# Two reductions of the second masked attention, moved in front of the dense attention's shares in VectorE's order

## The chip, the cores and the metric

The kernel runs on one core of a Trainium2 chip, with one launch. The metric is the time of one execution in device microseconds (us). Five engines work side by side, each through its own instructions in order: TensorE (PE; its weight loads are listed as PEld), VectorE (DVE), ScalarE (ACT), GpSimd (POOL) and SyncE (SP), which issues most of the DMA transfers. They wait for each other through semaphores.

## The reference

Sixteen batches of 1024 nodes with 256 features go through two layers of graph attention, each with a layer norm in front and a residual around it. Layer 0 holds an MLP, an attention over all nodes ("dense"), a second MLP and an attention masked by the adjacency matrix; layer 1 is one masked attention. Cut to what matters here:

```python
def _gat(inp, adj_mask, W, a):           # layer 0, slope 0.2; dense where adj_mask is None
    h = jnp.matmul(inp, W)
    f1, f2 = jnp.matmul(h, a[:F_, 0]), jnp.matmul(h, a[F_:, 0])
    e = jax.nn.leaky_relu(f1[:, :, None] + f2[:, None, :], ALPHA)
    if adj_mask is not None:
        e = jnp.where(adj_mask[None, :, :] > 0, e, NEG_INF)
    att = jax.nn.softmax(e, axis=2)
    return jax.nn.elu(jnp.einsum('bij,bjf->bif', att, h))
...
# layer 1, slope 0.01
h = jnp.matmul(inp, W)
e_src, e_dst = jnp.einsum('bnf,f->bn', h, a1), jnp.einsum('bnf,f->bn', h, a2)
e = jax.nn.leaky_relu(e_src[:, :, None] + e_dst[:, None, :], negative_slope=ALPHA)
e = jnp.where(adj[None, :, :] == 0, NEG_INF, e)
h_prime = jnp.matmul(jax.nn.softmax(e, axis=-1), h)
```

## The kernel before

**Order by a table.** All work is cut into small steps. Each step is entered in a table with a due time by `at(lo, hi, steps)`, which spreads the steps evenly from `lo` to `hi`. The due times are planned microseconds, and only their order counts: at the end the table is sorted by due time and the steps are issued one after the other, which fixes the order of instructions on PE, DVE, ACT and SP. POOL is kept in the same order by dependencies, with its scatters free among themselves. A step that issues nothing on an engine doesn't change that engine's order.

**Batches overlap.** Every batch `b` has a base, `base_of(b)`, 142 planned units after the one before (28 less from batch 1 on). Around one base the loop plans, for the middle batches: the layer 0 masked attention of batch `b` (`masked_first`, class `Gnn0`, tiles named with an a: `hma`, `exta`), the norm and the projections of the layer 1 masked attention of batch `b` (`second_norm`, class `Gnn1`, tiles named with a b: `hmb`, `extb`), the end of the dense attention of batch `b+1` (`dense_end`, class `Dense`), the first MLP and dense projections of batch `b+2`, and the first norm of batch `b+3`. The layer 1 attention proper (`masked_second`) comes one base later.

**The dense attention** doesn't multiply out its 1024 x 1024 weights (batch 0 does for half of its rows). The nodes are sorted by one of their two scores, sums from the front and from the back of the sorted rows are put into a fine and a coarse table in DRAM, and for every node POOL gathers one row of each table by an indirect DMA (L637; the coarse row is added to the fine one on landing). Per half of a batch (four tiles of 128 nodes) `share` (four DVE instructions, L649 to L652) makes the denominators from the gathered rows `got`. Then `mean`, once for each of the four tiles, scales the front sums on ACT (L659, tile `part`, two buffers) and adds the back sums on DVE (L661, tile `hp`). `merge` transposes the four `hp` tiles on PE (L708) for each of four column blocks, applies the first two steps of the elu on DVE and ACT (L710 to L712), and `merge_end` adds the result to `resT` (L718 on DVE, L719 on POOL).

**The layer 1 attention's preparation.** `project` multiplies each of eight node tiles with the weights on PE (L322) and copies the result from PSUM to `hmb` on ACT (L324). `extremes` reduces column 1 of `hmb`, the second scores, to their maximum and minimum for each partition (L329 and L330 on DVE, tile `ext`). `vectors` spreads the maximum over the partitions with a transpose on PE (L238, PSUM tile `extps`, from one of two `tr` buffers, which `merge` uses too), reduces it again on DVE (L339), and makes the exponentials of the attention on DVE and ACT (L341 to L351).

For a middle batch the order around the change, in planned units after `base_of(b)`: projections of layer 1 from 71 to 77.1; `share` of the first half at 78 and its four `mean` at 78.2, 78.575, 78.95 and 79.325; four steps of the first MLP (`mlp1`, L451, two products each, relu L454 on ACT) at 78.1, 79.85, 81.6 and 83.35; `extremes` at 78.5; `vectors` at 82; `merge` of the first half from 85, with projections of the dense attention (L465) between.

Of the kernel before, what the change touches and what calls it, by code (L numbers as in the profile page):

```python
# [31 lines left out]
def fast_path(ctx: ExitStack, tc: tile.TileContext, alarm, x, adj, w1, b1, w2, b2, w_fc, a_fc,  # L32
# [189 lines left out]
    def at(lo, hi, steps):  # L222
        for i, step in enumerate(steps):
            table.append((lo + (hi - lo) * i / len(steps), len(table), step))
# [543 lines left out]
    def each(f, *ranges):  # L768
        out = [()]
        for r in ranges:  # L770
            out = [o + (i,) for o in out for i in r]
        return [partial(f, *o) for o in out]
# [117 lines left out]
    def last(b, n=1):  # L890
        return b >= NB - n

    def second_norm(t0, b):
        n, m = norm2[b], gnn1[b]
        if last(b):
            n.turn_at(t0 + 46.5, 0)
            n.turn_at(t0 + 49, 1, 1.6)
            lo = t0 + 50
        elif b == 0:
            n.turn_at(t0 + 47, 0)  # L900
            n.turn_at(t0 + 50.5, 1, 1.6)
            lo = t0 + 47.2
        else:
            n.turn_at(t0 + 60.3, 0, 7)
            n.turn_at(t0 + 67.3, 1)
            lo = t0 + 71
        at(lo, lo + 7, each(m.project, range(NT)))
        at(lo + 7.5, lo + 7.5, [m.extremes])
        if last(b, 2):
            at(lo + 7.8, lo + 7.8, [m.vectors])  # L910
            at(lo + 8.2, lo + 8.2, [m.row])
            at(lo + 8.3, lo + 9.5, each(m.scale, range(NT)))
        else:
            at(lo + 11, lo + 11, [m.vectors])
            at(lo + 24, lo + 24, [m.send])
            at(lo + 40, lo + 52, each(m.scale, range(NT)))
            at(base_of(b + 1) - 4.5, base_of(b + 1) - 4.5, [partial(m.row, True)])
# [22 lines left out]
    def base_of(b):  # L940
        return b * PERIOD - SHORT * (b > 0)
# [37 lines left out]
    for t in range(TH):  # L979
        lo = START + 95 + 7.1 * t  # L980
# [31 lines left out]
    for b in range(NB):  # L1012
        base, after_base = base_of(b), base_of(b + 1)
        masked_first(base, b)
        second_norm(base, b)
        if last(b):
            parts = [base + 65 + 7 * q for q in range(NQ)]
        elif last(b, 2):
            parts = [base + 86, base + 94.5, base + 107.5, after_base + 39]
        else:  # L1020
            parts = [after_base + lo for lo in (11, 46, 53, 60)]
        masked_second(parts, b)
        if b + 1 < NB:
            if b:
                dense_sums(base, b + 1)
            for h in range(NH):
                if b:
                    gathers(dense[b + 1], h, base + 44.5 + 3.5 * h, base + 55 + 7 * h)
                else:
                    gathers(dense[1], h, base + 16 + 12 * h, base + 22 + 25 * h)  # L1030
            dense_end(after_base - PERIOD, b + 1)
        if b + 2 < NB:
            first_mlp(base, b + 2)
            dense_rows(after_base - PERIOD, b + 2)
            dense_begin(after_base, b + 2)
        if b + 3 < NB:
            lo = after_base - PERIOD + 86
            at(lo, lo, [partial(load_first, b + 3)])
            first_norm(after_base, b + 3)
# [465 lines left out]
```

## Time and profile before

| | |
|---|---|
| time, median of 4 runs | 2360.46 us (2358.52 to 2362.2) |
| profiled execution | 2356.86 us, its span 2355.1 us, granted clock 0.991 |
| PE busy | 2263.6 us, 96% |
| DVE busy | 1611.6 us, 68% |
| ACT busy | 1242.8 us, 53% |
| POOL busy | 954.3 us, 41% |
| two reductions of layer 1, L329 and L330 | 16 times each, 159 and 156 ns (medians) |
| the transpose of their result, L238 | 16 times, 294 ns (median) |

The span runs from the first to the last instruction of the program. The chain of waits, which follows the work that ended last back from the last instruction, is spread over many lines. Its largest shares are PE 8% and DVE 4%, and the largest line is L384, a product of the masked attention, with 2%. The table of waits is read as: the engine, tile and line that waited, the engine, tile and line (or DMA) that released it, the total, the number of times and the longest. The timeline gives the start and the duration in us of instructions of the same kind put together, with the idle time before them and its releaser in brackets. PE's rows have modelled ends. "Granted clock" is the share of TensorE's full clock that the chip's throttle let through.

### The profile page before, as it was taken

The numbers are of one execution on the slowest core, as the hardware profiler recorded it, in microseconds if no ns is written. First come the engines' busy times: TensorE is split into PE (matmuls) and PEld (weight loads), VectorE is DVE, ScalarE is ACT, GpSimd is POOL, SyncE is SP. The second block draws the span as 40 slices with busy tenths as digits, with TensorE's granted clock in tenths as the row PEclk, the third lists the DMA queues.
The fourth block names the chain that finished last, engine by engine and source line by source line (L and its number), as shares of the span: only waits on it lengthen the run. The fifth ranks groups of instructions, "written<-read, shape, count | busy, mean of one in ns | idle before, by whom it ended". The sixth has DMA issues, their size and how long they took to land. (4 is left out here: it accounts for less than half of the span.)

```text
span 2355.1 us, 30815 instructions
## 1 busy us (share of the span) xinstructions
PE 2263.6 (96%) x9955; PEld 1749.6 (74%) x9955; DVE 1611.6 (68%) x4499; ACT 1242.8 (53%) x2740; POOL 954.3 (41%) x1216
## 2 busy tenths in 40 slices
PE   8989999999999999999999999999999999999897
PEld 6667777777868778787777868777786877868666
DVE  6666685766858667775866868576685856768554
ACT  5345645547355563745547365564736556373442
POOL 1153435264433536335263533526443353634320
PEclk9999999999999999999999999999999999999899
DMA  4557346562655736366573645657265574636500
GB/s 173 168 155 212 72 162 179 163 186 91 199 133 175 184 136 182 100 185 163 169 196 104 194 116 165 176 168 191 97 197 120 175 184 145 181 90 202 127 1 29
DMA packets 150763, 355.81 MB, mean 151 GB/s; under 512 B 11113, under 2 KB 62649, under 8 KB 146497
## 3 DMA queue, kind: packets, MB, share of 16 engines
q0 software_dynamic: 45952, 163.99, 26.2%
q1 hardware_dynamic: 103968, 189.58, 26.2%
q8 instruction: 82, 1.34, 0.2%
q14 instruction: 89, 0.72, 0.1%
q10 hardware_dynamic: 672, 0.17, 0.0%
HBM read 227.40 MB, written 126.30 MB: 150 GB/s over the span
## 5 line engine op out<-in xcount | busy, mean ns | idle before, releaser
L384 PE MATMUL ob<-hmb,attb 128*128 128x257 f32 x2048 | 463.3, 384 | 13.8 <-DVE attb L373 13.8
L465 PE MATMUL h<-wfc_sb,resT 128*128 128x257 f32 x2048 | 465.8, 380 | 0.0
L384 PE MATMUL oa<-hma,atta 128*128 128x258 f32 x2048 | 455.8, 383 | 2.8 <-DVE atta L373 2.6
L384 PEld LDWEIGHTS ob<-hmb,attb 128*128 128x128 f32 x2048 | 386.2, 191 | 78.0 <-ACT rb L422 12.4
L384 PEld LDWEIGHTS oa<-hma,atta 128*128 128x128 f32 x2048 | 388.6, 190 | 64.7 <-DVE atta L373 8.0
L465 PEld LDWEIGHTS h<-wfc_sb,resT 128*128 128x128 f32 x2048 | 379.5, 190 | 53.5 <-issue 0.7
L719 POOL TENSOR_TENSOR resT<-resT,e 128x512 f32<-128x512 f32 x128 | 163.1, 1275 | 384.2 <-DVE e L718 340.9
L408 POOL TENSOR_TENSOR posa<-posa,onat 128x256 f32<-128x256 f32 x120 | 100.8, 840 | 469.2 <-ACT posa L400 468.6
L373 DVE SCALAR_TENSOR_TENSOR atta<-rowsa,qwda,edge 128x256 f32<-128x256 f32 x512 | 267.9, 553 | 25.6 <-PE oa L384 14.3
L373 DVE SCALAR_TENSOR_TENSOR attb<-rowsb,qwdb,edge 128x256 f32<-128x256 f32 x512 | 236.8, 505 | 8.4 <-PE ob L384 5.8
L451 PE MATMUL m<-hT,w_sb 128*128 128x512 f32 x512 | 237.3, 602 | 0.5 <-ACT posa L400 0.5
L726 PE MATMUL m<-resT,w_sb 128*128 128x512 f32 x512 | 231.2, 598 | 4.4 <-POOL resT L719 4.4
L422 ACT ACTIVATE rb<-ob,recb 128x256 f32<-128x256 f32 x128 | 59.0, 474 | 329.2 <-DVE recb L420 326.6
L637 POOL DMA_INDIRECT got<-coarse,k x124 | 198.0, 1597 | 38.5 <-issue 34.8
L399 ACT ACTIVATE ea<-oa,reca 128x256 f32<-128x256 f32 x128 | 60.7, 474 | 269.6 <-DVE reca L396 269.6
L710 DVE TENSOR_SCALAR e<-hpT 128x512 f32<-128x512 f32 x128 | 88.4, 690 | 139.4 <-PE hpT L708 106.9
L726 PEld LDWEIGHTS m<-resT,w_sb 128*128 128x128 f32 x512 | 94.1, 192 | 106.9 <-issue 91.2
L451 PEld LDWEIGHTS m<-hT,w_sb 128*128 128x128 f32 x512 | 93.4, 194 | 92.9 <-issue 90.6
L637 POOL DMA_INDIRECT got<-fine,k x124 | 128.9, 1040 | 54.1 <-issue 23.1
L525 POOL DMA_INDIRECT sorted<-hnat,place x128 | 131.4, 1026 | 39.6 <-issue 21.4
L548 ACT ACTIVATE junk<-r,fs 128x1024 int8<-128x1024 f32 x124 | 142.4, 1148 | 6.8 <-issue 3.6
L711 ACT ACTIVATE e<-e 128x512 f32<-128x512 f32 x128 | 80.7, 631 | 86.2 <-DVE e L710 86.1
(186 smaller groups left out, 3441.5 us busy)
## 6 DMA issues: line engine op xcount, KB each, us to landing
xs<-sorted SPq DMA_DIRECT2D x32, 1028.0 KB
fine<-tt SPq DMA_DIRECT2D x32, 1026.0 KB
fine<-xs SPq DMA_DIRECT2D x32, 1026.0 KB
x<-in_x_dram SPq DMA_DIRECT2D x16, 1024.0 KB
out_dram<-x SPq DMA_DIRECT2D x32, 512.0 KB
xn<-in_x_dram SPq DMA_DIRECT2D x15, 1024.0 KB
coarse<-carry SPq DMA_DIRECT2D x32, 256.5 KB
r<-row_r SPq DMA_DIRECT2D x14, 512.0 KB
```

The lines of the kernel that those rows point to most:

```text
L373: nc.vector.scalar_tensor_tensor(a_t, self.rows[:, q * PAIR:(q + 1) * PAIR], self.qwd[:, 1, j:j + 1], edge[:, j, q * PAIR:(q + 1) * PAIR], ...
L384: nc.tensor.matmul(self.out[t][:, :F + self.ONES], lhsT=self.att[q, j][:, (t % 2) * P:(t % 2 + 1) * P], rhs=self.hm[:, j, 2:2 + F + self.O ...
L408: adder.tensor_add(pos, pos, o_nat[:, t, :])
L451: nc.tensor.matmul(ps, lhsT=w1_sb[:, kc, c * P:(c + 1) * P], rhs=hT[:, kc, h * HALF:(h + 1) * HALF], start=(kc == 0), stop=(kc == FC - 1))
L465: nc.tensor.matmul(ps[:, :F + 1], lhsT=self.resT[:, kc, t * P:(t + 1) * P], rhs=wfc_sb[:, kc, g, :], start=(kc == 0), stop=(kc == HC - 1))
L525: made = nc.gpsimd.indirect_dma_start(out=sorted_d[self.b % 2], out_offset=bass.IndirectOffsetOnAxis(ap=self.place[:, t:t + 1], axis=0), i ...
L548: nc.scalar.activation(junk, self.r2, AF.Sign, bias=self.fs[:, 0, t:t + 1], accum_out=self.signs[:, t:t + 1])
L637: nc.gpsimd.indirect_dma_start(out=got[u // n][:, u % n, :], out_offset=None, in_=(coarse_d if coarse else fine_d)[self.b % 2][:, :], in_o ...
L710: nc.vector.tensor_scalar_min(e, ps, 0.0)
L711: nc.scalar.activation(e, e, AF.Exp)
L719: nc.gpsimd.tensor_add(dst, dst, e)
L726: nc.tensor.matmul(ps, lhsT=w2_sb[:, kc, c * P:(c + 1) * P], rhs=self.resT[:, kc, h * HALF:(h + 1) * HALF], start=(kc == 0), stop=(kc == H ...
```

## The change

The due time of `extremes` in `second_norm` goes from 7.5 to 6.9 units after `lo`, where `lo` is 71 units after the base for batches 1 to 14, 47.2 for batch 0 and 50 for batch 15. The projections that it reads keep due times up to 6.125 after `lo`. `extremes` of the layer 0 attention, planned in `second_mlp`, is not touched.

```diff
         at(lo, lo + 7, each(m.project, range(NT)))
-        at(lo + 7.5, lo + 7.5, [m.extremes])
+        at(lo + 6.9, lo + 6.9, [m.extremes])
         if last(b, 2):
             at(lo + 7.8, lo + 7.8, [m.vectors])
             at(lo + 8.2, lo + 8.2, [m.row])
```

## The prediction

> **What bounds the kernel.** I read the page first. TensorE (PE) is busy for 2263.6 of 2355.1 us, 96%, VectorE (DVE) for 68%; the chain of waits names mostly PE lines. So a change pays only where it shortens a PE wait, or what PE meets next. The table of waits (columns: engine, tile and line that waited, what released it; total us, times, longest) has two rows that bear on this step:
>
> ```profile
> DVE den L649 <- DMA got<-coarse,k: 133.6, 26, 10.7
> ...
> PE extpsb L238 <- DVE extb L330: 21.5, 14, 3.0
> ```
>
> PE waits 21.5 us for the second reduction of `extremes` (L330). Inside 300 to 2100 us it is 19.9 us in 12 waits, the largest PE row there; the next is 8.0 us. VectorE itself stands for 133.6 us at the first instruction of `share` (L649), waiting for gathered rows. The reductions are queued behind that. One round (batch 1) in the timeline, start and duration first:
>
> ```profile
> 378.59 5.31 PE L451 MATMUL m<-hT,w_sb 128*128 128x512 f32 x12
> 378.79 0.37 ACT L324 COPY hmb<-pb 128x258 f32<-128x258 f32 x1 [0.50 <-PE pb L322]
> ...
> 383.52 0.17 DVE L649 TENSOR_TENSOR den<-got,qd 128x4 f32<-128x4 f32 x1 [9.91 <-DMA got<-coarse,k]
> ...
> 385.08 0.75 DVE L661 SCALAR_TENSOR_TENSOR hp<-got,den,part 128x513 f32<-128x513 f32 x1 [0.79 <-ACT part L659]
> 385.75 0.16 DVE L329 TENSOR_REDUCE extb<-hmb 128x1 f32<-128x8 f32 x1
> 385.83 0.15 DVE L330 TENSOR_REDUCE extb<-hmb 128x1 f32<-128x8 f32 x1
> ...
> 386.06 0.29 PE L238 MATMUL extpsb<-ident,extb 128*128 128x128 f32 x1 [2.16 <-DVE extb L330]
> ```
>
> The last input of the reductions, ScalarE's (ACT's) copy at L324, is there at 379.16 (378.79 + 0.37). PE ends its twelve matmuls at 383.90, and sits 2.16 us. The next stretch decides the matter:
>
> ```profile
> 385.90 2.29 DVE L661 SCALAR_TENSOR_TENSOR hp<-got,den,part 128x513 f32<-128x513 f32 x3
> 386.19 1.88 PE L451 MATMUL m<-hT,w_sb 128*128 128x512 f32 x4
> ...
> 387.91 0.67 PE L708 MATMUL hpT<-ident,hp 128*128 128x128 f32 x4
> ```
>
> After the transpose of the extremes PE has one `mlp1` step (1.88 us), and then the transposes of `merge`, one for each `mean` result. The fourth result ends at 385.90 + 2.29 = 388.19, and the fourth transpose starts at 388.25. In twelve of the thirteen rounds of this kind (batches 1 to 13) it starts 0.05 to 0.07 us after that end. So PE reaches the two waits almost together: it is already bound by `mean` two microseconds later.
>
> **What the step moves.** Only two reductions, with no DMA and nothing on another engine. In batches 1 to 13 the new due time (77.9 instead of 78.5 after the base) puts them in front of four instructions of `share` (78.0) and one of `mean` (78.2). In batches 0, 14 and 15 no VectorE step lies between the two due times (in 14, `share` comes ten units later), so nothing changes there. On PE, ACT, POOL and SP the order stays.
>
> **Cost on VectorE.** The two take 0.16 and 0.15 us, overlapped 0.23. They gain a wait of their own, for the last copy of `project`. Behind it are queued `share` and `mean`, and PE waits for these. But the copy is done before the gathers in every round: 379.16 against 383.52 here, 1080.18 against 1082.34 in batch 6, the narrowest. VectorE is idle then. So the cost is nothing, hidden by the wait for the gathers; without that cover it would be 0.23 us a round, 3.0 us in all. Batch 14 shows the step with nothing in front: copy ready 2190.46, reduction 2190.49, PE's transpose 2190.80, so 0.34 us later. At 379.16 + 0.34 = 379.5 the extremes are ready 4.4 us before PE comes at 383.90. The wait at L238 goes wholly: 2.16, 2.06, 2.97, 1.00, 0.44, 0, 0.29, 1.47, 1.77, 1.99, 2.30, 1.93 and 1.56 us in batches 1 to 13, together 19.9.
>
> **What is late next.** PE runs its `mlp1` step from about 384.0 and is at `merge` at 385.9, two microseconds early. The results it transposes come from `share`, which the gathers release, and these don't move: in the stretch before it the DMA engines are full, as the row of the windows shows (us, busy time of PE, weight loads, DVE, ACT, POOL, then clock, DMA share, GB/s):
>
> ```profile
> 379.20:383.50 4.30, 4.30 (x11) 1.72 (x10) 0.00 (x0) 0.69 (x1) 2.40 (x3) 1.00 1.07 226
> ```
>
> What moves is only that the reductions no longer stand between the first `mean` and the second. From the start of the first to the end of the fourth that takes now 388.19 - 385.08 = 3.11 us. The nearest row without them is the other half, later in the same round, the same four instructions unbroken:
>
> ```profile
> 399.00 2.97 DVE L661 SCALAR_TENSOR_TENSOR hp<-got,den,part 128x513 f32<-128x513 f32 x4 [1.47 <-ACT part L659]
> ```
>
> 3.11 - 2.97 = 0.14 us. The reductions took 0.23, but the scale on ACT that feeds each `mean` sets the pace after the second. So the fourth transpose comes 0.14 us earlier, and the rest of the 2.16 is waited there. Over eleven rounds that is 1.5 us; batch 6, where PE came last anyway, gives nothing. What follows on VectorE (`vectors`, the minimum of `merge`) moves up by the same 0.14; the next waits of over 0.1 us that PE meets come in the following masked attention, and the first gather of the next round hangs on PE's own progress, so the gain is kept.
>
> **The thirteenth round: the clock.** In batch 3 the wait was 2.97 us, and the four matmuls after it took 3.13 us instead of 1.88. The windows say why:
>
> ```profile
> 661.80:665.20 3.40, 1.09 (x3) 0.19 (x1) 0.98 (x5) 1.07 (x2) 0.00 (x0) 1.00 1.05 223
> 665.20:668.60 3.40, 2.74 (x4) 1.28 (x5) 3.31 (x11) 2.97 (x6) 0.00 (x0) 0.50 1.05 221
> ```
>
> After 3.4 us with PE busy for 1.09, the granted clock (the third figure from the end) is 0.50 for the next 3.4 us. The transposes of `merge` start at 669.06, against 665.86 + 1.85 = 667.71 by batch 1's spacing: 1.35 us lost. Two more pairs of rows bound when this happens:
>
> ```profile
> 2238.73:2242.14 3.41, 1.56 (x4) 0.30 (x2) 1.70 (x4) 1.26 (x3) 2.19 (x2) 1.00 0.00 0
> 2242.14:2245.55 3.41, 2.91 (x4) 1.36 (x5) 0.00 (x0) 0.69 (x1) 0.54 (x3) 0.50 0.00 0
> 2317.23:2320.64 3.41, 1.73 (x12) 1.47 (x13) 2.15 (x10) 2.64 (x8) 0.00 (x0) 1.00 0.01 2
> 2320.64:2324.05 3.41, 3.41 (x17) 3.01 (x16) 3.41 (x10) 2.00 (x6) 0.00 (x0) 1.00 0.03 7
> ```
>
> 1.56 us of work in such a window leads to half clock, 1.73 does not. So about 1.7 us of idle time in one window is enough. [...] By the rows, six waits of 1.9 us and more are at risk, depending on where they fall in the windows. [...] After the change the idle time is 0.14 shorter and cut up by three transposes, so it falls into one window less easily; where it still does, the slow window lies over fully busy PE and costs 3.41/2 = 1.7 us. Bounds: batch 3 saved and one more spared, 2.7 us less; two extra slow windows, 3.4 us more. I take one slow window less, 1.35.
>
> **Sum.** 1.5 + 1.35 = 2.9 us, from a span of 2355.1 us that ran in 2356.86 us. That execution lies 3.6 us under the median of the runs, 2360.46, and under the lowest, 2358.52; slow windows in the others may be the reason, which can't be seen. From the median: **2357.6 us**, 0.12% less. A measurement of this kernel can hardly tell 0.2% (4.7 us) from no change.
>
> **Rivals.**
> 1. *The wait moves to `merge`* (my forecast), 2357.6; by itself 2355 to 2361. For it: the 0.05 to 0.07 us between the fourth `mean` and its transpose. Chance 0.53.
> 2. *The same, with the clock helping more.* If the runs with 2360 us hold three or four slow windows, and the cut-up idle time spares three, 1.5 + 3 x 1.35 = 5.6 us: 2354.9. For it: six waits over 1.9 us, and a median above the profiled execution. Against: one slow window alone in the steady part of the trace. Chance 0.27.
> 3. *The wait is really gone.* If the transposes had slack that the trace hides, PE would gain up to 19.9 us: 2340.6, or half of it, 2350. Against: the gathers' landing and the spacing at `merge`. Chance 0.08.
> 4. *Slower: slow windows at the new place.* The idle time now ends right before PE's densest stretch (13.60 of 13.60 us busy from 388.40). Each window halved there costs 1.7 us against 1.35; from the second extra window on the 1.5 us are eaten, and with five extra 5 x 1.7 - 1.5 = 7 us are lost: 2367.5. For it: round lengths near 139.7 us keep the waits at nearly the same place of the windows, so they hit or miss together. Against: shorter, divided idle time. Chance 0.12, most of it beyond 0.2%.
>
> That the reductions don't come earlier, since POOL's memset of the same tile (381.20, 0.70 us) came first, would still leave them ready at 382.2, before PE's 383.90; and in batch 6 of the first masked attention they ran at 1002.13, before that tile's memset at 1002.87.
>
> **Numbers.** Forecast 0.53, rivals 0.27, 0.08, 0.12. Faster: rival 2 for the most part and rival 3, with a little of 1, gives 0.34; slower 0.10; the same 0.56. The range reaches down to 2353.2, past rival 2, and up to 2361.6, the median plus some two extra slow windows less the 1.5.
>
> **What would show it.** L329 at about 379.2, before L649, with the wait at L238 gone from the PE rows for batches 1 to 13; in its place PE or its weight loads waiting for `hp` (L661) at L708, some 18 us; the four L661 in 2.97 us; DVE's wait for the gathers at about 133 us still. Wrong, if `merge` doesn't wait, if the gathers land at another distance from PE's projections, or if the windows at half clock in 300 to 2100 us become several.

## The result, and the profile after

The changed kernel takes 2357.78 us (median of 34 runs) against 2362.12 us of the kernel before on the same chips (55 runs): ratio 0.9983, 95% interval 0.9976 to 0.9991, so 0.17% or 4.0 us faster, between 2.1 and 5.7 (the two medians by themselves lie 4.3 us apart). The single runs scatter by some 16 us in both kernels (2354.31 to 2370.0 before, 2351.91 to 2369.28 after), so one profiled execution can't show a gain of this size: that of the changed kernel has the longer span, 2358.1 us against 2355.1. Its last part, in which the change moves nothing, took 294.8 us against 290.6, with 41.0 us at half clock against 33.1. From L339 of batch 1 to L339 of batch 13 it took 1675.4 us (387.90 to 2063.30) against 1676.5 (388.11 to 2064.58), but a second trace of the changed kernel took 1680.9 there, so that shows no gain either. The traces are read here for where PE waits, and the times are taken from the runs.

TensorE's waits between 300 and 2100 us in the changed kernel (what waited, what released it, total us, times, longest):

```profile
PE hpT L708 <- DVE hp L661: 13.2, 33, 0.7
PE ob L384 <- DVE attb L373: 7.3, 15, 0.8
```

The row of L238 with its 19.9 us is gone, and a row that wasn't there has come: the transposes of `merge` wait for `mean`. The weight loads in front of these transposes (PEld) show the same; in the kernel before they wait 0.3 us for `mean`, in the changed one:

```profile
PEld hpT L708 <- DVE hp L661: 19.8, 37, 0.7
```

VectorE's own waits in that stretch:

```profile
DVE extb L329 <- ACT hmb L324: 72.3, 13, 5.6
DVE den L649 <- DMA got<-coarse,k: 59.5, 24, 4.5
```

Together 131.8 us, where `share` alone waited 133.1: the reductions have cut VectorE's wait for the gathers in two, and not shortened it. Batch 1 in the timeline (start, duration, engine):

```profile
379.24 0.38 ACT L324 COPY hmb<-pb 128x258 f32<-128x258 f32 x1 [0.50 <-PE pb L322]
...
379.65 0.17 DVE L329 TENSOR_REDUCE extb<-hmb 128x1 f32<-128x8 f32 x1 [5.58 <-ACT hmb L324]
379.73 0.16 DVE L330 TENSOR_REDUCE extb<-hmb 128x1 f32<-128x8 f32 x1
...
383.46 0.16 DVE L649 TENSOR_TENSOR den<-got,qd 128x4 f32<-128x4 f32 x1 [3.57 <-DMA got<-coarse,k]
...
384.19 0.27 PE L238 MATMUL extpsb<-ident,extb 128*128 128x128 f32 x1
...
384.30 1.88 PE L451 MATMUL m<-hT,w_sb 128*128 128x512 f32 x4
...
385.02 2.97 DVE L661 SCALAR_TENSOR_TENSOR hp<-got,den,part 128x513 f32<-128x513 f32 x4 [0.79 <-ACT part L659]
...
386.02 0.27 PE L708 MATMUL hpT<-ident,hp 128*128 128x128 f32 x1
...
386.50 0.33 PE L708 MATMUL hpT<-ident,hp 128*128 128x128 f32 x1 [0.21 <-DVE hp L661]
...
387.38 0.33 PE L708 MATMUL hpT<-ident,hp 128*128 128x128 f32 x1 [0.56 <-DVE hp L661]
...
388.05 0.33 PE L708 MATMUL hpT<-ident,hp 128*128 128x128 f32 x1 [0.34 <-DVE hp L661]
```

The extremes are ready four microseconds ahead of PE, which runs on without a stop at 384.19 and through its `mlp1` step, and is at `merge` two microseconds earlier than before (386.02 against 387.91). There it goes from one `mean` to the next. The fourth transpose starts at 388.05, 0.06 us after the fourth `mean` ends (385.02 + 2.97 = 387.99); before it was 388.25 after 388.19, 0.06 too. In the changed kernel that holds in all thirteen rounds. The four `mean` take 2.97 us instead of 3.11.

### The profile page after: what moved, and what is told of

Its sections match the earlier page's. It is cut to its first block, busy times and chain, and to the rows that moved or that the text cites. A ratio compares the mean times of both kernels' runs of the same rounds, so it can differ in the third digit from the quotient of the medians.

```text
span 2358.1 us, 30828 instructions
## 1 busy us (share of the span) xinstructions
PE 2274.4 (96%) x9955; PEld 1755.9 (74%) x9955; DVE 1613.4 (68%) x4499; ACT 1242.6 (53%) x2740; POOL 956.0 (41%) x1216
## 5 line engine op out<-in xcount | busy, mean ns | idle before, releaser
L384 PE MATMUL ob<-hmb,attb 128*128 128x257 f32 x2048 | 467.7, 386 | 13.6 <-DVE attb L373 13.2
L465 PE MATMUL h<-wfc_sb,resT 128*128 128x257 f32 x2048 | 468.6, 382 | 0.0
L465 PEld LDWEIGHTS h<-wfc_sb,resT 128*128 128x128 f32 x2048 | 381.4, 191 | 54.2 <-issue 0.7
L525 POOL DMA_INDIRECT sorted<-hnat,place x128 | 131.8, 1030 | 39.5 <-issue 20.3
```

The lines of the kernel that those rows point to most:

```text
L384: nc.tensor.matmul(self.out[t][:, :F + self.ONES], lhsT=self.att[q, j][:, (t % 2) * P:(t % 2 + 1) * P], rhs=self.hm[:, j, 2:2 + F + self.O ...
L465: nc.tensor.matmul(ps[:, :F + 1], lhsT=self.resT[:, kc, t * P:(t + 1) * P], rhs=wfc_sb[:, kc, g, :], start=(kc == 0), stop=(kc == HC - 1))
L525: made = nc.gpsimd.indirect_dma_start(out=sorted_d[self.b % 2], out_offset=bass.IndirectOffsetOnAxis(ap=self.place[:, t:t + 1], axis=0), i ...
```

## The experiments

Each ratio is to the kernel before, run on the same chip. "Steady part" is the stretch from 300 to 2100 us, which holds the rounds of batches 1 to 13 (where a kernel is slow, the end of the thirteenth lies behind it). A window is a stretch of 3.41 us: in the traces of the kernel before and of the changed one the granted clock, between its first and its last change, keeps its value for a whole number of them.

**The changed kernel again**, as the neighbour of the next three.

> The changed kernel once more, as the neighbour of the next three. Theory (PE's wait moves from the extremes' transpose to the first transposes of merge, and only the 0.14 us by which the fourth mean ends earlier is kept, with perhaps a slow clock window less): ratio to before about 0.998, between 0.997 and 0.9995. A rival under which the whole wait is gone would show in the trace as no wait at merge and a ratio near 0.992.

2357.54 us, ratio 0.9978 (0.9967 to 0.9989). The result repeats; in this trace `merge` waits 15.1 us.

**One spare pair at the old place.**

```diff
         at(lo + 6.9, lo + 6.9, [m.extremes])
+        if 0 < b < NB - 2:
+            at(lo + 7.5, lo + 7.5, [partial(m.again, 1)])
...
+        def again(self, pairs):
+            f2 = self.hm[:, :, 1]
+            spare = small.tile([P, 2], F32, tag="spare", name=f"spare{self.name}")
+            for _ in range(pairs):
+                nc.vector.tensor_reduce(spare[:, 0:1], f2, AX.X, OP.max)
+                nc.vector.tensor_reduce(spare[:, 1:2], f2, AX.X, OP.min)
```

> The changed kernel, and in batches 1 to 13 the same two reductions once more at their old place between the first and the second mean, into a spare tile that nobody reads. PE doesn't wait for them. If the 0.14 us in the chain of means carries the gain: the four means take 3.11 us again, 11 to 13 x 0.14 = 1.5 to 1.8 us are lost, ratio to before about 0.999 and to the changed kernel about 1.0007. If the gain comes only from where PE idles (the clock), the ratio to before stays that of the changed kernel, 0.998.

2363.16 us, ratio 1.0006 (0.9992 to 1.0019). The four `mean` take 3.11 us again in every round, PE still doesn't wait at L238, and the gain is gone. So the gain hangs on the 0.14 us in the chain of `mean`; that PE waits at another place is worth nothing that can be measured. The size is another matter: 0.28% or 6.6 us against the run above, where 1.5 to 1.8 were expected. The two intervals leave some 4 us either way, so that even the least, 2.5 us, is more than the expected sum.

**Eight spare pairs**, `m.again` with 8.

> As before it, with eight such pairs at the old place: sixteen reductions at about 0.08 us each hold the second mean up by about 1.3 us. Theory (merge waits for the fourth mean, PE has no slack there): 13 x 1.3 = 17 us more than the changed kernel, about 2375 against 2358, ratio to before about 1.0055. If PE had slack at merge (rival), up to 2 us a round would be free and the time that of the changed kernel, ratio 0.998.

2394.07 us, ratio 1.0129 (1.0109 to 1.0148). PE has no slack at `merge`, so the rival falls. But the price is twice the expected one. The chain of `mean` grew from 2.97 to 4.52 us; 13 x 1.55 makes 20 us, and the kernel lost 36 against the first run. Two neighbouring windows of its trace (us, busy PE, weight loads, DVE, ACT, POOL, then granted clock, DMA share, GB/s):

```profile
384.99:388.40 3.41, 0.91 (x3) 0.34 (x3) 3.28 (x17) 1.92 (x4) 0.00 (x0) 1.00 1.09 228
388.40:391.81 3.41, 3.19 (x8) 2.63 (x9) 1.77 (x9) 2.98 (x7) 0.00 (x0) 0.51 1.04 222
```

PE works 0.91 us of one window while it waits at `merge`, and the next 3.4 us are granted half clock. There are nine such windows in the steady part and a tenth in the thirteenth round, at 2105.3 us, against one in the trace of the first run. Nine more, at up to 3.41/2 = 1.7 us each, are up to 15 us (an estimate): 20 + 15 is about the 36 measured.

**The reductions behind all four `mean`.**

```diff
-        at(lo + 7.5, lo + 7.5, [m.extremes])
+        at(lo + (8.4 if 0 < b < NB - 2 else 7.5), lo + (8.4 if 0 < b < NB - 2 else 7.5), [m.extremes])
```

> The kernel before, with the reductions of batches 1 to 13 not in front of share but behind all four means of the half. The chain of means takes 2.97 us, as in the changed kernel, but PE waits at the extremes' transpose until the fourth mean is done and has one mlp1 step (1.88 us) left before merge. Theory (both waits lie in a row on PE): merge starts about 2 us later than before, 13 x 2 = 26 us, ratio about 1.011. If the wait at the extremes' transpose costs PE nothing, because something later absorbs it (rival): ratio 1.000 or a little below.

2406.12 us, ratio 1.0189 (1.0164 to 1.0214): 43 us slower instead of 26. PE's wait in the steady part, and batch 1:

```profile
PE extpsb L238 <- DVE extb L330: 45.5, 12, 4.8
```

```profile
389.11 0.44 PE L238 MATMUL extpsb<-ident,extb 128*128 128x128 f32 x1 [4.80 <-DVE extb L330]
389.35 3.62 PE L451 MATMUL m<-hT,w_sb 128*128 128x512 f32 x4
392.76 0.98 PE L708 MATMUL hpT<-ident,hp 128*128 128x128 f32 x4
```

The wait is paid in full and the `mlp1` step after it once more before `merge` can start. In twelve of the thirteen rounds that step runs wholly or in part at half clock, here 3.62 us instead of 1.88. Where it ran at full clock (round 5) the fourth transpose came 2.40 us after the fourth `mean`, in the others 3.22 to 4.51. The steady part holds 47.8 us at half clock, against 3.4 in the kernel before; up to half of the difference, 22 us, is lost (an estimate), so there is room in it for the 17 us that the sum missed. The order of PE's two waits was understood, and the clock was left out.

**The gathers in another order.**

```diff
-                    gathers(dense[b + 1], h, base + 44.5 + 3.5 * h, base + 55 + 7 * h)
+                    gathers(dense[b + 1], h, base + 44.5 + 13.5 * h, base + 51.5 + 12 * h)
```

> The kernel before, with the gathers of a middle batch planned in another order on POOL: fine and coarse rows of the first half, then fine and coarse rows of the second half (before: fine, fine, coarse, coarse). Eight gathers instead of twelve then land ahead of the first share. Theory (what bounds PE at this place is the landing of the first half's coarse rows, whichever PE instruction meets it first): share starts some 8 us earlier, before the last projection, PE waits neither at the extremes' transpose nor at merge of the first half, 19.9 us and the slow clock windows of one to three are saved, unless the second half's merge takes the wait over: ratio between 0.990 and 0.994. Rival (DMA time isn't the bound, POOL or the means are): ratio 0.998 to 1.002.

> The changed kernel with the same order of gathers. Theory: where share isn't late, it doesn't matter what stands in front of it, so the change is worth nothing here: the same ratio to before as its neighbour without the change, within 0.1%. If the change has a value of its own (rival), it stays 0.2% ahead of its neighbour.

2399.27 us, ratio 1.0156 (1.0128 to 1.0184), and with the change 2399.3, 1.0158 (1.0136 to 1.0180). The hoped-for gain was a miss: slower by 1.6%. Its own condition says why. In batch 1 of the first of the two `share` starts at 378.46 instead of 383.52 (5 us earlier, not 8), and L238 has vanished from PE's waits, but the second half now holds PE (the three lines are from POOL's, VectorE's and PE's timelines):

```profile
380.14 1.58 POOL L637 DMA_INDIRECT got<-coarse,k  x1 [5.30 <-DMA got<-fine,k]
```

```profile
378.46 0.16 DVE L649 TENSOR_TENSOR den<-got,qd 128x4 f32<-128x4 f32 x1 [4.45 <-DMA got<-coarse,k]
```

```profile
402.72 0.30 PE L708 MATMUL hpT<-ident,hp 128*128 128x128 f32 x1 [2.58 <-DVE hp L661]
```

A coarse gather adds to the fine row, so POOL stands 5.30 us until the second half's fine rows have landed; its `mean` come later, `merge` of the second half waits, and 30.7 us of the steady part run at half clock. That the gathers bound the first half is confirmed. The second expectation agrees with the traces: at `merge` of the first half the four transposes run without a stop, and start 0.62 us after the fourth `mean` without the change and 0.76 us after it with the change, so PE comes last there, whatever stands in front of `share`. The times differ by 0.02% only, but their intervals leave some 0.36% either way, so by time alone a value of 0.2% isn't excluded.

**Ready work in front of `merge`.** One projection of the dense attention (L465, 1.9 us) is planned ahead of the first `merge`, in the kernel before and in the changed one:

```diff
-    BETWEEN = (86.0, 88.3, 90.6, 92.9, 94.7, 96.4, 97.5, 99.5)
+    BETWEEN = (84.9, 86.0, 88.3, 90.6, 92.9, 94.7, 96.4, 97.5)
```

> The kernel before, with the eight interleaved projections of the dense attention (L465) each one place earlier in the plan, so that one of them (1.9 us of PE work that is ready) stands in front of the first merge. PE meets the wait for the extremes first, with nothing to fill it, so about 20 us of waiting stay there and the projection only delays merge by the time that it later saves: ratio 0.998 to 1.003.

> The changed kernel with the projections one place earlier. Theory (the change moved PE's wait to merge, where work can be put in front of it): the projection covers most of the 13.6 us that merge's first transposes wait in the profile, and fewer windows run at half clock: 12 to 20 us less than the changed kernel, ratio to before 0.989 to 0.993. If the wait at merge is only apparent (rival), ratio 0.998 as for the change alone.

Without the change 2365.11 us, ratio 1.0006 (0.9993 to 1.0020); with it **2341.63 us, 0.9906 (0.9881 to 0.9930)**. First the waits at this place without the change, then batch 1 with it:

```profile
PE extpsb L238 <- DVE extb L330: 20.2, 12, 2.5
```

```profile
384.05 0.27 PE L238 MATMUL extpsb<-ident,extb 128*128 128x128 f32 x1
384.16 1.88 PE L451 MATMUL m<-hT,w_sb 128*128 128x512 f32 x4
385.88 1.90 PE L465 MATMUL h<-wfc_sb,resT 128*128 128x257 f32 x8
387.62 0.60 PE L708 MATMUL hpT<-ident,hp 128*128 128x128 f32 x4
388.06 1.90 PE L465 MATMUL h<-wfc_sb,resT 128*128 128x257 f32 x8
```

With the change, the projection fills the two microseconds in which PE would wait, and no window of the steady part runs at half clock. What `merge` still waits in this trace:

```profile
PE hpT L708 <- DVE hp L661: 2.2, 7, 0.4
```

Either edit alone gives 0.2% or nothing, both together 0.9%: as long as PE stands at the extremes' transpose, work placed behind it covers nothing.

**Four pairs, with and without that filling.** Does a delay cost more than its length because of the clock, or because the reductions disturb something?

> The changed kernel with four spare pairs of reductions at the old place: by the first two runs of this kind the four means take 2.97 + 0.15 + 3 x 0.2 = 3.7 us, 0.75 us more a round, 9.8 us over thirteen. Theory A (a delay costs PE its own length): about 2367.5, ratio to before 1.002. Theory B (a longer wait at merge also brings windows at half clock, so that a delay costs some 1.8 times its length, as with eight pairs: 36 us for 20): about 2375, ratio 1.0055, and several windows at half clock between 300 and 2100 us.

> The same four pairs in the kernel with the change and the projections one place earlier (2341.6, ratio 0.9906 without the pairs). There PE waits at merge for at most 0.7 us, so even with 0.75 us more no window of 3.4 us loses half its work to it. Theory B: the pairs cost their own length only, less what PE comes late in rounds 1 and 4 to 7 there: some 6 to 8 us, ratio about 0.9935, no window at half clock between 300 and 2100 us. Theory A': the factor comes from elsewhere (the reductions themselves disturb), then they cost as much here as beside the change alone, 0.6 to 0.75%.

Beside the change alone 2376.38 us, ratio 1.0038 (1.0018 to 1.0059); in the filled kernel 2349.88 us, 0.9940 (0.9912 to 0.9967). The chain of `mean` is 3.72 us in both. PE's wait for `mean` at `merge` (the line numbers are 7 higher, by the added function), first without the filling (a further 3.9 us at `merge` are put down to the spare reductions, L337), then with it:

```profile
PE hpT L715 <- DVE hp L668: 19.7, 34, 1.0
```

```profile
PE hpT L715 <- DVE hp L668: 7.3, 14, 0.8
```

Without the filling, four windows of the steady part run at half clock, and the pairs cost about 0.58% (against 0.998), 13.7 us for 9.8 us of delay, with some 5 us either way. With it one does, where none was expected, and they cost 0.34%, 8 us, as the sum of their own length expected, but with some 9 us either way. The interval of the first holds the figures of both theories (1.002 and 1.0055), and that of the second doesn't exclude the 0.6% of the other theory, so by the time alone the case is open; the windows, and the eight pairs, speak for the clock.

## Why the prediction was right

- *PE is already bound by `mean` two microseconds later.* Shown: the fourth transpose keeps its distance of 0.06 us, and eight pairs of reductions there cost all of their length and more. The expected row, some 18 us at L708 for PE or its weight loads, is there with 19.8 us for the weight loads and 13.2 to 15.1 us for PE.
- *The reductions cost nothing in front of `share`.* Shown: 379.65 against 383.46 in batch 1, VectorE's two waits together as long as the one before.
- *0.14 us a round are kept.* Shown in the trace (2.97 for 3.11), and by one spare pair, which takes the 0.14 and the gain away together.
- *One slow window less, 1.35 us.* Not shown. The kernel before has one in the steady part of its trace, the changed one two and, repeated, one. The reason given for it, that the idle time, cut up by three transposes, falls into one window less easily, failed too. In batch 2 of the changed kernel the pieces were 0.69, 0.27 and 0.56 us, PE is shown busy for 1.90 of 3.42 us, more than the 1.73 that I took to be safe, and half clock followed all the same:

```profile
523.75:527.17 3.42, 1.90 (x6) 0.56 (x4) 2.48 (x5) 3.00 (x5) 0.00 (x0) 1.00 1.08 229
527.17:530.58 3.41, 3.18 (x8) 2.33 (x9) 2.13 (x9) 2.99 (x8) 0.00 (x0) 0.50 1.08 228
```

- *The sum.* 2.9 us forecast, 4.0 measured (2.1 to 5.7). That they are close is in part luck: nearly half of the 2.9 is the slow window that isn't shown, and the 1.5 us alone lie below the interval. So is the nearness of 2357.6 to the measured 2357.78, since the median of the kernel before moved from 2360.46 in four runs to 2362.12 in 55. That waits of 1.9 us and more are at risk was rightly read from the rows of the windows: in batch 2 above even 1.5 us in pieces of 0.69 us at most were followed by a window at 0.50. But the rows were used for one window more or less, and not as something that makes a delay dearer. The runs show that for a long delay: 36 us for 20 with eight pairs. With four pairs it was 13.7 for 9.8, and 8 us where PE has work, both within wide intervals. With the 1.8 of the eight pairs the 0.14 us in twelve rounds would be worth 3.0 us. That is an estimate; nothing shows that the factor holds for so short a delay, and where the rest of the 4.0 us comes from stays open, since windows counted in single traces don't resolve it.
- *The rivals.* The wait that is really gone fell: PE waits at `merge`, and eight pairs there were paid in full. That the clock helps more, 5.6 us, lies just inside the interval; the slow windows in the traces (one before, two and one after) don't speak for it. That more slow windows come at the new place, enough to lose, fell for this change. Longer delays at this place did bring such windows: ten in the thirteen rounds with the eight pairs, and half clock in twelve of the thirteen with the reductions behind all four `mean`.

## What to carry to other kernels

A wait in the table is worth only the distance to what the same engine meets next (here 19.9 us of waits went, and 4.0 us were gained): before removing it, look some instructions further on that engine and compare their start with the end of what they need. Two waits in a row for the same late source (here the landing of the gathers) pay only once; take the first away and then put ready work in front of the second (0.94% here, against 0.17% without that work). Work that sits between the late source and the bound engine is on the path: here 0.14 us of it a round, put back by one spare pair, took the gain away.

## What was unexpected of the hardware

In batch 2 of the changed kernel PE lost its full clock without standing still for long: pieces of 0.27 to 0.69 us, 1.5 us in one window of 3.4 us, were followed by half clock (the rows above), at a cost of up to 1.7 us (an estimate: half of the 3.41 us at half clock). The busy time that the profile shows doesn't tell by itself which clock follows. In the kernel with the projections moved alone a window with 1.48 us was followed by full clock, and in the changed kernel with the gathers in another order one with 2.01 us by half clock:

```profile
380.84:384.25 3.41, 1.48 (x4) 0.38 (x2) 1.50 (x8) 1.38 (x3) 0.00 (x0) 1.00 1.08 228
384.25:387.67 3.42, 3.28 (x12) 2.19 (x13) 3.08 (x11) 3.20 (x8) 0.00 (x0) 1.00 1.05 220
```

```profile
1829.36:1832.77 3.41, 2.01 (x9) 1.36 (x10) 3.28 (x6) 2.57 (x7) 0.43 (x1) 1.00 0.01 1
1832.77:1836.19 3.42, 3.42 (x11) 2.42 (x10) 0.67 (x2) 1.73 (x3) 0.84 (x1) 0.50 0.00 0
```

Cut into windows of 3.413 us from the clock's first change on, the traces of the kernel before and of the changed one together hold 1056 windows at full clock between 300 and 2112 us. Three of them were followed by half clock, with PE shown busy for 1.12 us (from 661.77 us on, in the kernel before), 1.90 and 1.95 us (from 523.75 and 1503.38 us on, in the changed kernel). The other 1053 were followed by full clock, and the least busy of them shows 1.94 us (from 1361.50 us on, in the kernel before). A transpose that stands alone at full clock is shown with 0.27 to 0.33 us, where four in a stream take 0.60 us together, and that may blur the picture; whether it does isn't shown.

So in this kernel a delay of PE by 1.55 us a round cost 2.8 us a round (36 us in all). Half that delay, 0.75 us a round in the kernel that keeps PE busy, cost about its own length, 8 us for 9.8, within a wide interval.
